# A place of its own in PSUM for the decay of each of two groups, instead of a ring of two

## The chip, the core and the metric

The kernel runs on one core of a Trainium2 chip, as one program. The time is device microseconds of that core; the metric is the median of several executions. One further execution was taken with the hardware profiler on, and what is said of instructions comes from that one.

## What is computed

Two layers work on 16 images of 64 x 64 pixels with 96 channels. The first layer normalizes by groups of channels, widens the image, applies two matrices with a square between them, and filters it back. The second layer is a state space layer, and nearly all of the time passes in its scan. Cut to what matters here:

```
delta = softplus(dts + bias)                    # per direction k, channel d, position l
h[l]  = exp(delta[l] * A[k,d,n]) * h[l-1] + delta[l] * u[l] * B[n,l]
y[l]  = sum over n of C[n,l] * h[l]             # 16 states n, 4 directions k, 192 channels d
```

`exp(delta * A)` is called the decay below, and `delta * u * B` the drive.

## The kernel before, in words

The scan is cut into *units*. A unit holds two groups, `e = 0` and `e = 1`; a group is 128 partitions (32 channels by 4 states) by 1024 positions in float32. Six blocks of channels, each with four sets of states (`j = 0` to `3`), make 24 units for a stretch of 1024 positions; four stretches, in two pairs of directions, make 192 units for an image, and 16 images make 3072 units. The units run in one long loop (L916), written out in full. The order of the instructions on each engine is the order in which the code names them (a manual schedule); the framework puts in the semaphores.

For each unit `n` and group `e`, these are the steps:

- `decay` (L785): ScalarE (ACT) writes `da = exp(delta * a)` into a tile of the PSUM pool `sc_aps`. A tile is 4 KB in each partition, two banks. Each `da` is a new tile.
- `drive` (L791): GpSimd (POOL) makes both groups' drive `b` in SBUF with one multiplication (L794). The tile `b` has four places.
- `recur` (L797): VectorE (DVE) runs the recurrence as one scan instruction over `da` and `b` (L803, or L805 where the direction is reversed). Its result goes either over `b` or over `da`.
- The result is multiplied by C. For group 0, DVE does it (L972, out of `da` into `b`). For group 1, POOL does it (L963, inside `b`), except in every fifth unit (`odd_here`, L948), where the scan's result stays in `da` and DVE does it (L954). These are called *fifth units* here. In some stretches a counter (`full_unit`) puts them closer together, and then leaves them out for a while.
- `keep` (L807): the last column is copied as the start of the next stretch, by DVE or ACT (L811).
- `read_out` (L813): TensorE (PE) sums over the states (L827).

In the loop the order for unit `n` is: scan of group 1, [fifth unit: DVE's multiplication], copy, **decay of (n+1, 1)**, POOL's multiplication of group 1, drive of n+2, scan of group 0, DVE's multiplication of group 0, copy, **decay of (n+1, 0)**. So while unit `n` is at work, the decays of unit `n+1` are made.

The PSUM pool `sc_aps` has two places (banks 2 and 3, banks 4 and 5). They are a common ring: each new `da`, of either group, takes a place that the framework picks when it lays out the program, and waits at run time for the last reader of the tile that had the place before.

Beside the scan, two *background* programs are put into the loop in slices: `front` of the next image (first layer, normalizations, convolution) and `finish` of the image before; and `project` of the next stretch. They use mostly PE and ACT, and a little DVE. In the last image there is no `front`.

Of the kernel before, what the change touches and what calls it, by code (L numbers as in the profile page):

```python
# [45 lines left out]
F32 = mybir.dt.float32  # L46
# [3 lines left out]
PSUM = bass.MemoryType.PSUM  # L50
# [12 lines left out]
T = 1024  # L63
# [17 lines left out]
def tile_two_blocks(  # L81
# [541 lines left out]
    def scan():  # L623


        with ExitStack() as es:
# [142 lines left out]
                    if (what, 0, j) not in bc:  # L769
                        bc[what, 0, j] = fetch_bc(ctxs[0], 0, j, what)  # L770
            banks.append(es.enter_context(tc.tile_pool(name="b_ps", bufs=2, space=PSUM)))
            aps = es.enter_context(tc.tile_pool(name="sc_aps", bufs=2, space=PSUM))
            yps = es.enter_context(tc.tile_pool(name="sc_yps", bufs=1, space=PSUM))
            gps = es.enter_context(tc.tile_pool(name="sc_gps", bufs=1, space=PSUM))

# [2 lines left out]
            def group(n, e):  # L778
                st, bi, _ = units[n]
                v, s0, r = blocks[bi]  # L780
                return 2 * steps[st][1] + r, s0 + e if v < 2 else 4 + e
# [2 lines left out]

            def decay(n, e):  # L785
                k, g = group(n, e)
                da = aps.tile([128, T], F32, name="da")
                nc.scalar.activation(da, deltas[n // NQ, e], AF.Exp, scale=a_s[:, k, g, units[n][2]:units[n][2] + 1])  # L788
                das[n, e] = da

# [121 lines left out]
            for e in range(2):  # L912
                decay(0, e)
            storing, credit = None, 0

            for n, (st, bi, j) in enumerate(units):  # L916
# [39 lines left out]
                if n < last:  # L956
                    decay(n + 1, 1)
# [16 lines left out]
                if n < last:  # L974
                    decay(n + 1, 0)
# [25 lines left out]
    with tc.manual_schedule():  # L1001
        with tc.tile_pool(name="first_ps", bufs=8, space=PSUM) as pool:
            banks.append(pool)
            for _ in front(0):
                pass
            banks.pop()
        scan()
        with tc.tile_pool(name="last_ps", bufs=8, space=PSUM) as pool:
            banks.append(pool)
            for _ in finish(B - 1):  # L1010
                pass
            banks.pop()
# [95 lines left out]
```

## Time and profile before

| | |
|---|---|
| median of 3 runs | 21318.96 us (21314.29 to 21335.73) |
| profiled execution, its own time | 21326.15 us |
| its span, first to last instruction | 21324.4 us |
| DVE busy | 19510.9 us, 91% |
| POOL busy | 19511.8 us, 91% |
| PE busy | 16949.4 us, 79%, at a mean granted clock of 0.859 |
| ACT busy | 13759.8 us, 65% |
| first scan starts, last scan ends | 495.9 us, 21158.7 us |

A row of the profile's groups gives the line, the engine, the operation, the tile written and the tiles read with their sizes, how often; then the busy time in us and the mean duration in ns; then the engine's idle time ahead of these instructions, and whose end it waited for. A row of the waits gives who waited for whom, the total in us, how often, and the longest. A row of the timeline gives start and duration in us, and in brackets the idle time ahead of it.

### The profile page before, as it was taken

How to read it: one execution, taken by the hardware profiler on the slowest of the kernel's cores; microseconds unless marked ns; L12 is line 12 of the kernel's file. 1: busy time of each engine (PE TensorE's matmuls, PEld its weight loads, DVE VectorE, ACT ScalarE, POOL GpSimd, SP SyncE). 2: the span in 40 equal slices, each digit the busy share in tenths (PEclk: the TensorE clock that was granted, in tenths of full speed). 3: DMA queues.
4: the chain of work that ended last, by engine and by line, in shares of the span. 5: the costliest groups of instructions: out<-in, count | busy, mean ns of one | idle time of the engine just before them, and what ended most of it. 6: DMA issues, size and time to landing. Idle time of an engine off the chain costs nothing. (4 is left out here: it accounts for less than half of the span.)

```text
span 21324.4 us, 273404 instructions
## 1 busy us (share of the span) xinstructions
PE 16949.4 (79%) x98988; PEld 7262.1 (34%) x98988; DVE 19510.9 (91%) x12983; ACT 13759.8 (65%) x20546; POOL 19511.8 (91%) x5538
## 2 busy tenths in 40 slices
PE   7876788887878778787887888878787787878855
PEld 4423324233343333324333342333433333243221
DVE  0999999999999999999999999999999999999997
ACT  4666666666666666666666666666666666666553
POOL 0999999999999999999999999999999999999996
PEclk8887888888889888898888888888898888988977
DMA  2565565655656566565665656556565665656654
GB/s 83 184 204 188 198 225 191 219 197 197 223 195 226 189 211 210 192 230 184 218 205 197 223 194 219 198 193 223 195 227 188 212 209 193 230 188 216 222 187 140
DMA packets 1855464, 4277.11 MB, mean 201 GB/s; under 512 B 449438, under 2 KB 548670, under 8 KB 1852062
## 3 DMA queue, kind: packets, MB, share of 16 engines
q1 hardware_dynamic: 1854110, 4259.62, 59.5%
q8 instruction: 781, 12.80, 0.3%
q14 instruction: 573, 4.69, 0.1%
HBM read 3380.58 MB, written 878.18 MB: 200 GB/s over the span
## 5 line engine op out<-in xcount | busy, mean ns | idle before, releaser
L794 POOL TENSOR_TENSOR b<-dtu,bt 128x2048 f32<-128x2048 f32 x3072 | 13908.5, 4537 | 593.7 <-DMA dtu<-dtu_d 468.4
L788 ACT ACTIVATE da<-delta,a_s 128x1024 f32<-128x1024 f32 x6144 | 6846.5, 1116 | 3074.8 <-DVE b L972 947.3
L963 POOL TENSOR_TENSOR b<-b,ct 128x1024 f32<-128x1024 f32 x2458 | 5809.4, 2363 | 1052.8 <-DVE new L811 786.2
L827 PE MATMUL y<-b,fold_s 128*32 128x256 f32 x49152 | 3871.0, 438 | 1122.9 <-DVE b L972 663.2
L972 DVE TENSOR_TENSOR b<-da,ct 128x1024 f32<-128x1024 f32 x3072 | 3756.5, 1223 | 91.8
L803 DVE TENSOR_TENSOR_SCAN da<-da,new,b 128x1024 f32<-128x1024 f32 x1383 | 3246.6, 2348 | 206.5 <-ACT da L788 198.8
L805 DVE TENSOR_TENSOR_SCAN da<-da,new,b 128x1024 f32<-128x1024 f32 x1361 | 3194.1, 2347 | 200.8 <-ACT da L788 188.6
L827 PEld LDWEIGHTS y<-b,fold_s 128*32 128x32 f32 x49152 | 1394.5, 119 | 3847.4 <-issue 1492.7
L805 DVE TENSOR_TENSOR_SCAN b<-da,new,b 128x1024 f32<-128x1024 f32 x943 | 2208.1, 2342 | 112.8 <-ACT da L788 81.0
L803 DVE TENSOR_TENSOR_SCAN b<-da,new,b 128x1024 f32<-128x1024 f32 x921 | 2156.3, 2341 | 10.5 <-ACT da L788 9.9
L811 ACT COPY new<-da 128x1 f32<-128x1 f32 x2764 | 432.9, 157 | 2568.8 <-DVE b L972 2178.3
L488 PE MATMUL c_ps<-xgp,wtap_s 96*64 96x512 f32 (+1 forms) x4608 | 1721.4, 632 | 180.4 <-ACT row L506 175.1
L697 PE MATMUL s<-w,ident_s 128*128 128x512 f32 x1530 | 1166.9, 854 | 722.4 <-ACT w L692 618.0
L371 PE MATMUL h_ps<-xu,w1t_s 96*128 96x500 f32 x1920 | 1053.7, 646 | 362.2 <-ACT sd L362 185.5
L383 PE MATMUL o_ps<-w2c_s,hsq 128*100 128x96 f32 x9600 | 1044.3, 267 | 207.3 <-ACT hsq L352 206.9
L805 DVE TENSOR_TENSOR_SCAN da<-da,b 128x1024 f32<-128x1024 f32 x482 | 1103.8, 2290 | 106.7 <-ACT da L788 98.9
L677 PE MATMUL s<-pr,dtw_s 128*128 128x512 f32 x1530 | 937.8, 697 | 302.0 <-ACT delta L703 214.5
L803 DVE TENSOR_TENSOR_SCAN da<-da,b 128x1024 f32<-128x1024 f32 x460 | 1053.5, 2290 | 107.1 <-ACT da L788 106.9
L383 PEld LDWEIGHTS o_ps<-w2c_s,hsq 128*100 128x100 f32 x9600 | 979.0, 179 | 447.8 <-ACT hsq L352 263.2
L820 PE MATMUL y<-y,ident_s 128*128 128x512 f32 x768 | 532.2, 781 | 627.3 <-ACT yt L838 501.7
L697 PE MATMUL s<-e,ident_s 128*128 128x512 f32 x1530 | 1014.5, 752 | 0.0
L488 PEld LDWEIGHTS c_ps<-xgp,wtap_s 96*64 96x64 f32 (+1 forms) x4608 | 582.9, 169 | 1115.4 <-issue 849.2
(143 smaller groups left out, 21887.5 us busy)
## 6 DMA issues: line engine op xcount, KB each, us to landing
dtu<-dtu_d SPq DMA_DIRECT2D x1536, 512.0 KB
delta<-delta_d SPq DMA_DIRECT2D x1536, 512.0 KB
bt<-rows SPq DMA_DIRECT2D x1024, 512.0 KB
ct<-rows SPq DMA_DIRECT2D x1024, 512.0 KB
u<-xs_d SPq DMA_DIRECT2D x893, 256.0 KB
dtu_d<-dtu SPq DMA_DIRECT2D x765, 256.0 KB
delta_d<-delta SPq DMA_DIRECT2D x765, 256.0 KB
xr<-in_x SPq DMA_DIRECT2D x768, 128.0 KB
```

The source lines that it names most:

```text
L371: nc.tensor.matmul(h_ps[j], lhsT=w1t_s[:, 128 * j:128 * (j + 1)], rhs=xu.rearrange("c p q -> c (p q)"), start=True, stop=True,)
L383: nc.tensor.matmul(o_ps[:, p, :], lhsT=hsq[j][:, UPS * p:UPS * (p + 1)], rhs=w2c_s[:, j, :], start=(j == 0), stop=(j == HB - 1),)
L488: nc.tensor.matmul(c_ps[p:p + n], lhsT=wtap_s[:, tap, 128 * i:128 * i + n], rhs=xgp[:, h0:h0 + 8, dx:dx + HW], start=(tap == 0), stop=(tap ...
L677: nc.tensor.matmul(s, lhsT=dtw_s[:, pair, v, :], rhs=pr, start=True, stop=True)
L697: nc.tensor.matmul(s, lhsT=ident_s, rhs=of, start=(k == 0), stop=(k == 3))
L788: nc.scalar.activation(da, deltas[n // NQ, e], AF.Exp, scale=a_s[:, k, g, units[n][2]:units[n][2] + 1])
L794: nc.gpsimd.tensor_mul(b, dtus[n // NQ], bt.unsqueeze(1).to_broadcast([128, 2, T]))
L803: nc.vector.tensor_tensor_scan(out, da, b, before, ALU.mult, ALU.add)
L805: nc.vector.tensor_tensor_scan(out[:, ::-1], da[:, ::-1], b[:, ::-1], before, ALU.mult, ALU.add)
L827: nc.tensor.matmul(y[32 * q:32 * q + 32, e, :], lhsT=fold_s, rhs=b[:, e, QT * q:QT * q + QT], start=(pair == 0 and j == 0 and e == 0), sto ...
L963: nc.gpsimd.tensor_mul(h, h, bc[1, r, j])
L972: nc.vector.tensor_mul(bs[n][:, 0, :], h, bc[1, r, j])
```

## The change

The pool `sc_aps` gets one place for each tag instead of two in all, and the tile `da` gets the tag `da0` or `da1` after its group. That is again two places of two banks. A decay of group 0 now always waits for the last reader of the decay of group 0 before it, and a decay of group 1 for that of group 1.

```diff
-            aps = es.enter_context(tc.tile_pool(name="sc_aps", bufs=2, space=PSUM))
+            aps = es.enter_context(tc.tile_pool(name="sc_aps", bufs=1, space=PSUM))
...
             def decay(n, e):
                 k, g = group(n, e)
-                da = aps.tile([128, T], F32, name="da")
+                da = aps.tile([128, T], F32, name="da", tag=f"da{e}")
                 nc.scalar.activation(da, deltas[n // NQ, e], AF.Exp, scale=a_s[:, k, g, units[n][2]:units[n][2] + 1])
```

## The prediction

> **What bounds the kernel now.** I read the page's first part, then the groups of instructions, the waits, the timeline of two neighbouring units, and the busy time by stretch. First the busy time:
>
> ```profile
> PE 16949.4 (79%) x98988; PEld 7262.1 (34%) x98988; DVE 19510.9 (91%) x12983; ACT 13759.8 (65%) x20546; POOL 19511.8 (91%) x5538
> ```
>
> DVE and POOL are equally busy. The scan lasts from 495.9 to 21158.7 us, 20663 us, so each of them is idle there for some 1150 to 1250 us; that is all that a better order could bring. Who waits for whom decides between the two:
>
> ```profile
> L803 DVE TENSOR_TENSOR_SCAN da<-da,new,b 128x1024 f32<-128x1024 f32 x1383 | 3246.6, 2348 | 206.5 <-ACT da L788 198.8
> L805 DVE TENSOR_TENSOR_SCAN da<-da,new,b 128x1024 f32<-128x1024 f32 x1361 | 3194.1, 2347 | 200.8 <-ACT da L788 188.6
> L805 DVE TENSOR_TENSOR_SCAN da<-da,b 128x1024 f32<-128x1024 f32 x482 | 1103.8, 2290 | 106.7 <-ACT da L788 98.9
> L803 DVE TENSOR_TENSOR_SCAN da<-da,b 128x1024 f32<-128x1024 f32 x460 | 1053.5, 2290 | 107.1 <-ACT da L788 106.9
> ```
>
> Ahead of scans that write over `da` (all of group 0, and group 1 of fifth units) DVE idles 198.8 + 188.6 + 98.9 + 106.9 = 593 us until a decay is ready: half of its idle time. It rarely waits for POOL's drive (under 60 us in all groups of scans). POOL does wait for DVE:
>
> ```profile
> POOL b L963 <- DVE new L811: 786.2, 367, 18.3
> ```
>
> So DVE sets the pace in most of the scan, and POOL follows close behind. The timeline shows how the 593 us come about (rows of DVE and ACT; between them others are left out):
>
> ```profile
> 9992.10 2.34 DVE L803 TENSOR_TENSOR_SCAN b<-da,new,b 128x1024 f32<-128x1024 f32 x1
> ...
> 9992.42 1.12 ACT L788 ACTIVATE da<-delta,a_s 128x1024 f32<-128x1024 f32 x1
> ...
> 9994.55 2.35 DVE L803 TENSOR_TENSOR_SCAN da<-da,new,b 128x1024 f32<-128x1024 f32 x1
> ...
> 9998.08 2.34 DVE L803 TENSOR_TENSOR_SCAN b<-da,new,b 128x1024 f32<-128x1024 f32 x1
> ...
> 9998.78 0.17 ACT L811 COPY new<-da 128x1 f32<-128x1 f32 x1
> 10000.45 0.15 DVE L811 COPY new<-b 128x1 f32<-128x1 f32 x1
> 10000.45 1.12 ACT L788 ACTIVATE da<-delta,a_s 128x1024 f32<-128x1024 f32 x1 [1.50 <-DVE b L803]
> ...
> 10001.60 2.36 DVE L803 TENSOR_TENSOR_SCAN da<-da,new,b 128x1024 f32<-128x1024 f32 x1 [1.00 <-ACT da L788]
> ```
>
> These are units 1405 and 1406. In the first, the decay of group 0 runs at 9992.42, beside the scan of group 1, and the scan of group 0 follows at once. In the second, ACT is free from 9998.95, yet waits 1.50 us for the end of the scan of its own unit's group 1. Only then does the decay of group 0 run, while DVE stands still for 1.00 us. In the program as built the reason is the place: in unit 1406 the decay of group 0 was given the place that group 1 of the *same* unit holds. I call such units crossed. Going through all 3070 units from the third on, 527 are crossed; in 2543 each group takes its own place.
>
> **The change, part by part.** *What moves.* The order on every engine is the same, and so are the waits of PE, POOL and SP. Of 6144 decays, 527 wait for something else: instead of the scan of (n, 1) they wait for DVE's multiplication of (n-1, 0) and ACT's copy behind it. The multiplication stands ahead of that scan on DVE, and the copy ahead of the decay on ACT. The other 527 decays that lose a foreign place, those of group 1 right behind a crossed decay, now wait for the scan of their own group in the unit before; but ACT comes to them only after the crossed decay, which had waited for that scan already. So no wait on another engine becomes later. On DVE 22 scans get an additional wait for an earlier instruction of DVE itself, on ACT some decays one for the copy just ahead; I cost both at nothing, since the 2543 units of the ordinary kind have the same wait.
>
> *What it removes.* DVE's idle time ahead of the scan of group 0, summed over the 527 crossed units, is 557.7 us (1.06 us each); over the 2543 others it is 31.6 us (0.01 us each). So the trace holds the changed state in four units of five, and at most 557.7 - 527 x 0.0124 = 551 us go.
>
> *What stays of it.* In 54 of the 527 (105.8 us) the decay starts more than 0.06 us after the scan's end: there it waits for `delta` from DRAM (14 units, 51.0 us) or ACT is still at other work. These stay. In the other 473 (451.9 us) the scan's end released it. For each I took the later of the end of ACT's instruction before it and the end of the multiplication of (n-1, 0), added 1.12 us, and compared with the end of the scan of group 1. Mostly the decay would be done in time; where ACT is behind, 89 us remain. That leaves 452 - 89 = 363 us.
>
> *What is late next: POOL.* DVE can only be ahead of POOL as far as the four places of `b` reach: in the long runs without a fifth unit, POOL's L963 starts 4.3 us behind the scan and the next drive ends 0.03 us before its scan. There POOL sets the pace, since POOL's ordinary unit takes 4.53 + 2.36 = 6.89 us (rows L794, L963) and DVE's 2.34 + 2.35 + 1.22 + 0.15 = 6.06. It catches up in fifth units (4.53 against 7.15). A bubble of DVE that goes is time won only where POOL idles nearby. In windows of 24 units, the sum of the smaller of the two (crossed idle time, POOL's idle time ahead of L963 and L794) is 480 of 551 us; in windows of 5 units 333 of 551. A lag of 4.3 us spans a few bubbles, so the truth lies between the shares 0.87 and 0.60; I take 0.8, nearer to the long window, as about nine in ten of the crossed units lie outside the long runs. 363 x 0.8 = 290 us.
>
> The SBUF row that speaks against it: 32 instructions of L237 (96x1) average 3614 ns and 16 of L260 2391 ns, where L259 of nearly the same shape takes 146 ns. With POOL idling less they could each wait out a whole drive: 32 x (4.53 - 3.61) + 16 x (4.53 - 2.39) = 64 us at most, nothing at least. I take nothing, as POOL is busy 94% of the scan already, and keep the 64 us for the upper end. The Trainium skill ("SBUF — State Buffer", Who interferes with whom) says that a DVE instruction with two SBUF inputs contends with a GpSimd instruction that reads SBUF, and with one SBUF input it does not; by that rule L237 and L260 pay, and the scans, with `da` in PSUM, never do. The trace agrees: the scans take 2.33 to 2.36 us throughout.
>
> *The sum.* 21326 - 290 = 21036 us for an execution like the profiled one; it lies 7 us above the median of the runs, so 21319 - 290 = 21029, rounded to **21030 us**, 1.4% less. A measurement of this kernel can tell about 0.2%, 43 us, from no change.
>
> **The rivals.**
>
> 1. *POOL hides nothing, ACT is never late: all 529 to 551 us go.* Then about 20780. For it: the ordinary units idle 0.01 us, and ACT, no longer held, would also be earlier for what follows. Against: 89 us were ACT's own lateness, and in the long runs POOL has no lead to give. Chance 0.10.
>
> 2. *POOL or ACT eats more than two thirds, but not all.* Two windows of units:
>
> ```profile
> core 0: us, PE busy (x) PEld busy (x) DVE busy (x) ACT busy (x) POOL busy (x), PEclk, DMA share, GB/s
> ...
> 9573.30:10866.00 1292.70, 1050.53 (x6169) 453.01 (x6170) 1210.84 (x807) 851.77 (x1277) 1214.08 (x345) 0.87 0.61 205
> 19922.00:21161.00 1239.00, 770.05 (x3916) 257.64 (x3920) 1207.13 (x800) 675.40 (x950) 1217.03 (x346) 0.76 0.55 188
> ```
>
> These are an image with `front` beside it and the last one without. The last has 8 crossed units instead of some 35 and takes 1239 us, with POOL busy 1217 of it. So an image can lose 54 us at most before POOL is full; 35 bubbles are 37 us of that, and the rest of the 54 belongs to waits that stay. If POOL's idle time is mostly of a kind that DVE's pace doesn't govern, a third of 290 us is left: 21220. Chance 0.08.
>
> 3. *POOL is the bound: no change.* POOL is busiest by 0.9 us, and if its own chain (drive, multiplication, drive) ran through, DVE's bubbles would only turn into waits for `b`: 21319, within 43 us. Against it stand the 786.2 us in which POOL waits for DVE's copy. The Trainium skill ("Perfetto Trace Analysis", Identifying the Most-Contended Engine) has the busiest engine optimized first; by it the change would be worth nothing here, which this row speaks against. Chance 0.06.
>
> 4. *PE becomes the bound: slower.* The granted clock is 0.87 in the one stretch and 0.76 in the other. If the closer packing brought the images with `front` down to 0.76, PE's 1050 us would become 1050 x 0.87 / 0.76 = 1202 of an image's 1275 (1293 less 18 won). POOL waits 98 us in all today for PE's sums to free a `b`; then a `read_out` in line behind a late `front` matmul would hold `drive`. It decides once PE's busy time and its waits pass 1293 us per image: 100 us more of waits would give 1202 + 100 = 1302, nine above today, 15 x 9 = 135 us, so 21450. Against it: the lower clock stands where PE has less to do, not more. Chance 0.03; with one more in 100 for what I don't see, slower has 0.04.
>
> **How the numbers follow.** The forecast's own case, 20840 to 21200, has 0.72. Its lower end is the 363 us without POOL's share plus most of the 106 us of other lateness (21319 - 480); its upper end is the share 0.60 on 363 us, less 64 us for L237 and L260, and rounded down by a quarter for ACT falling behind as DVE's pace rises (21319 - 120). The range adds a little of rivals 1 and 2 at each end: 20820 to 21210. Faster than 21276 is 0.72 + 0.10 + 0.08 = 0.90; within 43 us 0.06; slower 0.04.
>
> **What would show it.** In the changed profile the idle time of the four groups that write over `da` should fall from 593 to about 200 us or less; no decay should show an idle time ended by the scan of group 1 of its own unit; the timeline of unit 1406 should look like that of 1405. DVE's waits for POOL's drive (L794) should rise from under 60 us to 100 or more, and POOL's wait for DVE (786.2 us) should fall by some 300. DVE and POOL busy times and the scan's duration stay within a few tenths of a per cent. I am wrong about the mechanism if the 593 us go and the span stays (rival 3), or if they stay; wrong about the size if POOL's wait falls by less than 150 us.

## The result, and the profile after

The changed kernel takes 21086.31 us (median of 4 runs, 21075.62 to 21088.51), against 21320.87 us for the kernel before (4 runs). The ratio is 0.9888, with a 95% interval of 0.9871 to 0.9905: 234.6 us less (234 in what follows), where 290 us were forecast and 20820 to 21210 us was the range. The profiled execution has a span of 21083.6 us, 240.8 us shorter than before.

The busy line of the page of the profile after:

```profile
PE 16908.7 (80%) x98988; PEld 7230.6 (34%) x98988; DVE 19569.4 (93%) x12983; ACT 13780.9 (65%) x20546; POOL 19498.8 (92%) x5538
```

The groups of scans that write over `da`, from the groups of DVE after (busy us, mean ns, idle us ahead of them and whose end it waited for):

```profile
L803 DVE TENSOR_TENSOR_SCAN da<-da,new,b 128x1024 f32<-128x1024 f32 x1383 | 3245.3, 2347 | 72.7 <-ACT da L788 57.2 <-POOL b L794 13.3
L805 DVE TENSOR_TENSOR_SCAN da<-da,new,b 128x1024 f32<-128x1024 f32 x1361 | 3193.0, 2346 | 99.7 <-ACT da L788 77.0 <-POOL b L794 21.0
...
L805 DVE TENSOR_TENSOR_SCAN da<-da,b 128x1024 f32<-128x1024 f32 x482 | 1103.5, 2289 | 53.0 <-ACT da L788 43.1 <-POOL b L794 9.2 <-ACT new L811 0.6
L803 DVE TENSOR_TENSOR_SCAN da<-da,b 128x1024 f32<-128x1024 f32 x460 | 1053.0, 2289 | 36.8 <-ACT da L788 34.8 <-POOL b L794 0.9 <-ACT new L811 0.2
```

The idle time that ends with a decay has fallen from 593 us to 57.2 + 77.0 + 43.1 + 34.8 = 212 us. The scans themselves last what they lasted, to a few ns. But DVE is busy for 58.5 us more, and parts of the idle time now end with POOL's drive. In the list of waits, POOL still waits for DVE, 158 us less than the 786.2 us of before, and PE waits longer for POOL's product:

```profile
POOL b L963 <- DVE new L811: 628.6, 296, 14.1
PE y L827 <- POOL b L963: 167.1, 136, 5.3
```

Before, that row of PE was:

```profile
PE y L827 <- POOL b L963: 133.8, 110, 5.5
```

The timeline of the same two units, 1405 and 1406, in the profile after:

```profile
9868.05 2.34 DVE L803 TENSOR_TENSOR_SCAN b<-da,new,b 128x1024 f32<-128x1024 f32 x1
...
9868.35 1.12 ACT L788 ACTIVATE da<-delta,a_s 128x1024 f32<-128x1024 f32 x1
...
9870.49 2.35 DVE L803 TENSOR_TENSOR_SCAN da<-da,new,b 128x1024 f32<-128x1024 f32 x1
...
9874.01 2.34 DVE L803 TENSOR_TENSOR_SCAN b<-da,new,b 128x1024 f32<-128x1024 f32 x1
...
9874.92 1.12 ACT L788 ACTIVATE da<-delta,a_s 128x1024 f32<-128x1024 f32 x1
...
9876.46 2.35 DVE L803 TENSOR_TENSOR_SCAN da<-da,new,b 128x1024 f32<-128x1024 f32 x1
```

Both units now look alike: the decay of group 0 starts while the scan of group 1 runs (9874.92, the scan ends at 9876.35), and DVE goes from scan to scan.

An account of the 240.8 us, from the groups of DVE in both traces (every gap is counted, also those under 0.15 us, which the rows of the profile leave out of their releasers). L702 is a multiplication of `project` that reads PE's sums, L578 one of `finish`; L237 and L260, which come up below, are small instructions of `front`, on 96x1 and 96x96 numbers.

| DVE | before, us | after, us | difference |
|---|---|---|---|
| all scans' idle time ended by a decay | 718.2 | 339.2 | -379.0 |
| all scans' idle time ended by POOL | 60.3 | 109.7 | +49.4 |
| busy | 19510.9 | 19569.4 | +58.5 |
| L702's idle time, nearly all until PE is done | 319.8 | 345.7 | +25.9 |
| L578's idle time, nearly all until ACT is done | 111.7 | 120.9 | +9.2 |

The sum is -236 us; 5 us are spread over the rest. In DVE's busy time the one group that grew is L237, from 115.6 to 195.0 us (records of neighbouring instructions overlap a little, so that the busy time grows by less). Its row before and after:

```profile
L237 DVE TENSOR_TENSOR nb<-nmean,rg 96x1 f32<-96x1 f32 x32 | 115.6, 3614 | 303.4 <-ACT rg L234 295.4 <-ACT new L811 8.1
```

```profile
L237 DVE TENSOR_TENSOR nb<-nmean,rg 96x1 f32<-96x1 f32 x32 | 195.0, 6095 | 301.9 <-ACT rg L234 294.2 <-ACT new L811 7.6
```

So the ring's bubbles (the idle time of DVE ahead of crossed scans) went as counted, and 143 us came back in four places. That L702's part comes from POOL, by way of PE's longer wait for POOL's product (133.8 to 167.1 us), is argued from these sums and not shown one by one. Where in an image they came back I took from the starts of the first scan of each part, for the 14 images from the second to the fifteenth:

| units of an image | idle time in crossed units, before and after | time won |
|---|---|---|
| 0 to 71 | 235.9, 58.7 us | 180.1 us |
| 98 to 149 | 242.3, 114.9 us | 17.7 us |
| the others | 40.1, 0.8 us | 12.8 us |

In the first part (units 0 to 71) as much time was won as idle time went (177 us gone, 180 won). In the later part (units 98 to 149) 127 us went and 18 were won. This is a balance of unlike places. In units 96 to 101, 18 us of waits for a decay went, but L237 grew by 52 us, and these units took 35 us longer. In units 120 to 125, 28 us went, and the waits for POOL's drive grew by 28 us and that of L702 by 18. In units 132 to 137, 28 us went and 30 were won.

POOL's idle time fell by about what was won: from 394 to 221 us in the first part, from 591 to 574 us in the later one (14 images). So POOL had more idle time in the later part than in the first, and hardly any of it went.

### The profile page after: what moved, and what is told of

Same layout as the page of the kernel before. It is cut to its first block, busy times and chain, and to the rows that moved or that the text cites. A ratio compares the mean times of both kernels' runs of the same rounds, so it can differ in the third digit from the quotient of the medians.

```text
span 21083.6 us, 273452 instructions
## 1 busy us (share of the span) xinstructions
PE 16908.7 (80%) x98988; PEld 7230.6 (34%) x98988; DVE 19569.4 (93%) x12983; ACT 13780.9 (65%) x20546; POOL 19498.8 (92%) x5538
## 5 line engine op out<-in xcount | busy, mean ns | idle before, releaser
L963 POOL TENSOR_TENSOR b<-b,ct 128x1024 f32<-128x1024 f32 x2458 | 5797.1, 2358 | 836.9 <-DVE new L811 628.6
L803 DVE TENSOR_TENSOR_SCAN da<-da,new,b 128x1024 f32<-128x1024 f32 x1383 | 3245.3, 2347 | 72.7 <-ACT da L788 57.2
L805 DVE TENSOR_TENSOR_SCAN da<-da,b 128x1024 f32<-128x1024 f32 x482 | 1103.5, 2289 | 53.0 <-ACT da L788 43.1
L803 DVE TENSOR_TENSOR_SCAN da<-da,b 128x1024 f32<-128x1024 f32 x460 | 1053.0, 2289 | 36.8 <-ACT da L788 34.8
```

What stands on the lines that cost most here:

```text
L803: nc.vector.tensor_tensor_scan(out, da, b, before, ALU.mult, ALU.add)
L805: nc.vector.tensor_tensor_scan(out[:, ::-1], da[:, ::-1], b[:, ::-1], before, ALU.mult, ALU.add)
L963: nc.gpsimd.tensor_mul(h, h, bc[1, r, j])
```

## The experiments

The theory was: a bubble of DVE is time only where POOL has idle time near it; elsewhere POOL is late already, and DVE meets POOL's lag (how far POOL is behind DVE's scans) at the next place where it depends on it. The first half of it does not fit the sums above, as POOL had idle time near the bubbles of both parts; the second half, that POOL takes the time back at the places where DVE depends on it, is what e3 to e6 test. The first rival was that each crossed unit costs the same, 234 / 527 = 0.44 us; further rivals belong to single runs.

To cross chosen units, the places were written out. `PLACE` takes the other place for group 0 of a unit unless the unit is in `CROSSED`; with all 527 units in it, the places are those of the kernel before, one by one:

```diff
+CROSSED = set(...)
+PLACE = {(0, 0): 0, (0, 1): 1, (1, 1): 1}
+for _n in range(1, 3072):
+    PLACE[_n, 0] = PLACE[_n, 1] if _n in CROSSED else 1 - PLACE[_n, 1]
+    PLACE[_n + 1, 1] = 1 - PLACE[_n, 0]
...
-                da = aps.tile([128, T], F32, name="da", tag=f"da{e}")
+                da = aps.tile([128, T], F32, name="da", tag=f"da{PLACE[n, e]}")
```

**e1, the 272 units of the first part crossed again.**

> Own places as in the changed kernel, except that the 272 units that were crossed in units 0 to 71 of an image (of 527) are crossed again. Theory 1 (a crossed unit costs time only where POOL idles nearby): these are the stretches that won nearly all, 180 us over 14 images in the two traces, so about 195 us over the whole come back: 21086 + 195 = 21280 us. Rival (each crossed unit costs the same, 234 / 527 = 0.44 us): 21086 + 272 x 0.44 = 21207 us.

Measured: 21291.74 us (10 runs), 0.9988 of the kernel before (0.9979 to 0.9997). 205 us are back, 0.75 us for each unit. The rival's 21207 us is out of reach.

**e2, the 215 units of the later part crossed again.**

> Own places, except that the 215 units that were crossed in units 98 to 149 of an image are crossed again. Theory 1: this stretch won only 18 us over 14 images although 157 us of DVE's idle time went there, since a second loss took it back (DVE's L237 behind a busier POOL, waits for the drive): 21086 + 20 = 21105 us, and L237's mean falls back from 6.1 us towards 3.6. Rival (same price everywhere): 21086 + 215 x 0.44 = 21181 us.

Measured: 21086.37 us (0.9889, 0.9874 to 0.9904), the changed kernel's time to a tenth of a microsecond. These 215 crossed units cost nothing in sum (that the two agree so closely is chance, as the runs of e2 lie between 21072.88 and 21099.99 us). The profile says how; its groups of the two instructions that gave way, and one group of scans:

```profile
L805 DVE TENSOR_TENSOR_SCAN da<-da,new,b 128x1024 f32<-128x1024 f32 x1361 | 3193.5, 2346 | 174.1 <-ACT da L788 159.2 <-POOL b L794 10.9 <-ACT new L811 2.6
...
L702 DVE TENSOR_TENSOR dtu<-s,u 128x512 f32<-128x512 f32 x765 | 520.7, 681 | 279.7 <-PE s L697 278.3 <-DMA dtu<-dtu_d 0.3 <-issue 0.3
L237 DVE TENSOR_TENSOR nb<-nmean,rg 96x1 f32<-96x1 f32 x32 | 140.8, 4400 | 302.5 <-ACT rg L234 294.9 <-ACT new L811 7.6
```

Against the changed kernel, the idle time ended by a decay is up by 126 us over all scans (465.3 against 339.2; the first row shows 82 of it). In return L237 is down from 195.0 to 140.8 us, L702's wait from 345.7 to 287.9 and the scans' wait for POOL from 109.7 to 88.4: 133 us. DVE waits about the same time in sum, only for something else. The two runs together show that the price of a crossed unit depends on its place: 0.75 us on average in one part, none on average in the other. Within the later part it differs as much: against the changed kernel, in 14 images, units 96 to 101 take 35 us less and units 120 to 125 19 us less, but units 132 to 137 30 us more. The expected times came from the same two profiles, so these runs confirm where the time is won, and not yet why. (The 157 us of idle time in e2's expectation are not what the traces give: it is 127 us in 14 images, 140 us in all 16.)

**e3 and e4, L237 on ACT.** The largest single group that grew was L237, a multiplication of 96 numbers at which DVE and POOL meet. The timelines of DVE and of POOL around the same instruction of the program (the 26th of 32), in the kernel before:

```profile
15429.10 2.29 DVE L237 TENSOR_TENSOR nb<-nmean,rg 96x1 f32<-96x1 f32 x1 [0.22 <-ACT rg L234]
...
15424.04 4.54 POOL L794 TENSOR_TENSOR b<-dtu,bt 128x2048 f32<-128x2048 f32 x1
15429.01 2.36 POOL L963 TENSOR_TENSOR b<-b,ct 128x1024 f32<-128x1024 f32 x1 [0.43 <-POOL b L794]
15431.33 9.01 POOL L794 TENSOR_TENSOR b<-dtu,bt 128x2048 f32<-128x2048 f32 x2
```

and in the kernel after:

```profile
15244.41 12.32 DVE L237 TENSOR_TENSOR nb<-nmean,rg 96x1 f32<-96x1 f32 x1 [0.22 <-ACT rg L234]
...
15240.96 4.53 POOL L794 TENSOR_TENSOR b<-dtu,bt 128x2048 f32<-128x2048 f32 x1
15245.43 2.38 POOL L963 TENSOR_TENSOR b<-b,ct 128x1024 f32<-128x1024 f32 x1
15247.74 8.96 POOL L794 TENSOR_TENSOR b<-dtu,bt 128x2048 f32<-128x2048 f32 x2
```

Before, POOL had begun its L963 0.09 us ahead of L237, and both ended together (15431.37 and 15431.39). After, POOL was a drive behind, had three more instructions in line without a gap, and L237 ended at 15256.73, with the last of them (15256.70). So DVE can wait for several instructions of POOL here. In 30 of the 32 places POOL was at work, and there, in both kernels, L237 ended 0.01 or 0.02 us after an instruction of POOL. After the change POOL then had nothing ready each time, for 2.5 us or more: DVE paid POOL's whole lag. Before, that was so 24 times; the other six times, the one shown here among them, POOL's next instruction followed without a gap. What let L237 through there stays open. Both kernels were run with that line on ACT:

```diff
-        nc.vector.tensor_mul(nb, nmean, rg)
+        nc.scalar.activation(nb, nmean, AF.Identity, scale=rg)
```

> The kernel before, with its places kept unit by unit, but L237 (nb = nmean * rg, 32 times) on ACT instead of DVE. Its 115.6 us on DVE (3.6 us each) become about 0.2 us each on ACT. Theory: DVE had to wait for POOL there, so 80 to 110 us go: about 21225 us. Rival (POOL sets the pace anyway at those places): no change, 21320 us.

> The changed kernel, with L237 on ACT as well. There L237 took 195.0 us (6.1 us each), 79 us more than before the change. Theory (L237 took back part of the gain): 21086 less 150 to 190 us, 20900 to 20935 us, and the distance to e3_nb_ring is 234 + 79 = about 310 us. Rival (the lead that POOL owes is only paid elsewhere, as waits for the drive): the distance stays at 234 us, about 20990 us.

Measured: e3 (places as before) 21183.84 us, 0.9937 (0.9921 to 0.9954); e4 (own places) 20929.54 us, 0.9815 (0.9801 to 0.9830). e3 gains 135 us, more than the 115.6 us that L237 had on DVE; e4 gains 157 us, less than its 195.0 us. The distance between the two is 254 us, near the rival's 234 and not my 310. L237 was a place where POOL's lag was collected. Without it, e4 pays elsewhere: against e3 its scans wait 117.0 us instead of 57.0 for POOL, and L702 351.9 instead of 322.8. L260, the other small instruction that the prediction had named, pays too. It had 38.3 and 38.1 us in the kernels before and after, and its rows in e3 and then in e4 are:

```profile
L260 DVE TENSOR_TENSOR lin<-lin,ident_s 96x96 f32<-96x96 f32 x16 | 52.9, 3303 | 0.0
```

```profile
L260 DVE TENSOR_TENSOR lin<-lin,ident_s 96x96 f32<-96x96 f32 x16 | 73.3, 4582 | 0.0
```

From e3 to e4, in 14 images, units 96 to 101, where L237 had grown by 52 us, win 17 us instead of losing 35; units 120 to 125, with the waits for the drive and of L702, lose 18 us instead of 9.

**e5 and e6, POOL relieved.** If it is POOL's lag, then less work for POOL must bring out the whole of the bubbles. In both kernels, half of one multiplication on POOL is left out:

```diff
-                    nc.gpsimd.tensor_mul(h, h, bc[1, r, j])
+                    nc.gpsimd.tensor_mul(h[:, 0:T // 2], h[:, 0:T // 2], bc[1, r, j][:, 0:T // 2])
```

> The kernel before with POOL relieved: L963 multiplies 512 of the 1024 columns only (the other half of group 1 keeps the unmultiplied scan, so the output is not the reference's). POOL's unit falls from 6.9 to about 5.7 us, below DVE's 6.1. Places as in the kernel before. DVE loses its waits for the drive (60 us) and part of L237's 116 us: about 21150 to 21250 us by both theories.

> The changed kernel with POOL relieved in the same way (half of L963's columns left out). Theory (POOL, by its lag and through L237, ate what is missing between the 379 us of idle time that went and the 241 us of the span): with POOL out of the way the distance to e5_half_ring is the full idle time, 350 to 390 us. Rival (ACT's own lateness or other waits ate it): the distance stays at about 235 us.

Measured: e5 (ring) 21159.65 us, 0.9924 (0.9909 to 0.9938); e6 (own places) 20763.40 us, 0.9737 (0.9721 to 0.9753). The distance is 396 us instead of 234, a little above the 350 to 390 expected. All idle time ended by a decay falls by 352 us from one to the other, L702's by 14. DVE's busy time falls by 26 us, though the durations of its instructions sum to the same: without a gap, the records of neighbours overlap more. The units that had taken time back no longer do: in 14 images units 96 to 101 win 18 us and units 120 to 125 16. The groups of POOL's second multiplication, e5 and then e6:

```profile
L963 POOL TENSOR_TENSOR b<-b,ct 128x512 f32<-128x512 f32 x2458 | 3125.6, 1272 | 3374.6 <-DVE b L803 1579.4 <-DVE new L811 903.7 <-DVE b L805 369.6
```

```profile
L963 POOL TENSOR_TENSOR b<-b,ct 128x512 f32<-128x512 f32 x2458 | 3122.7, 1270 | 2994.9 <-DVE b L803 1327.6 <-DVE new L811 837.5 <-DVE b L805 358.0
```

POOL now idles 3.0 to 3.4 ms ahead of it, 2.5 to 2.9 ms of that until DVE is done; the scans wait 3.6 and 2.6 us for it, and L237 takes 0.8 and 1.0 us. With POOL out of the way the change is worth about what DVE's bubbles sum to, and a little more by the overlap. What is missing in the full kernel is POOL's.

**e7 to e10, another share of the work.** In the kernel before, every fifth unit gives the multiplication of group 1 to DVE. If POOL now sets the pace more often, the balance should move (L237 stays on ACT):

```diff
-SHARE = 5
+SHARE = 6        # e7;  4 in e8 and e9 (e9 with the common ring), 3 in e10
```

> As e4_nb_own, but every sixth instead of every fifth unit leaves group 1's multiplication to DVE: 102 multiplications go from DVE (1.07 us more there than the copy it saves) to POOL (2.36 us). If DVE sets the pace nearly everywhere: up to 110 us faster than e4, 20820 us. If POOL sets it: up to 241 us slower, 21170 us. By the traces both do, in turns (DVE in units 0 to 71, POOL in units 150 to 168), so between 20880 and 21000 us.

> As e4_nb_own, but every fourth unit: 154 multiplications go from POOL to DVE. DVE gets 165 us more work, POOL 362 us less. If DVE sets the pace: up to 165 us slower than e4, 21095 us. If POOL sets it: faster. By the traces DVE sets it in the larger part, so 20950 to 21090 us.

Measured: e7 20958.11 us (0.9834, 0.9817 to 0.9850), 29 us more than e4 and within what was expected. e8 20868.95 us (0.9791, 0.9776 to 0.9805): 61 us *faster* than e4, where I had expected it slower. DVE's busy time rises only from 19411.5 to 19504.3 us, as L260 falls from 73.3 to 21.8 us, and its idle time shrinks by more: the waits for a decay from 348.4 to 309.9 us, those for POOL from 117.0 to 49.6 us, that of L702 from 351.9 to 291.2. So POOL set the pace in more of the kernel than the traces had told me.

> As e8_share4 (every fourth unit, L237 on ACT), but with the common ring of two. As built, 455 units are crossed instead of 527. If the ring's bubbles and POOL's lag stand in for one another, then with POOL relieved the bubbles cost more each than in e3 against e4 (254 us for 527, 0.48 us each): 455 x 0.65 = about 300 us above e8, 21165 us. If POOL's work plays no part in it: 455 x 0.48 = 219 us above e8, 21090 us.

> As e8_share4, but every third unit: 256 more multiplications go from POOL to DVE, 274 us more work for DVE. If POOL still set the pace with every fourth, faster than e8; if DVE does now, up to 274 us slower. DVE should: 20950 to 21140 us.

Measured: e9 21139.02 us (0.9913, 0.9896 to 0.9929), 270 us above e8 for 455 crossed units, 0.59 us each. That lies between the two expectations (219 and 300 us) and does not decide between them; it fits a price that rises when POOL has less to do, but other units are crossed here. e10 21187.91 us (0.9938, 0.9923 to 0.9952), 319 us more than e8, where at most 274 us more were expected. From e8 to e10 the span grows by 310 us and DVE's busy time by 313 us: DVE is the bound with every third unit. The multiplications (L954) alone took 313 us more, and L260 25 us. e8 is the best of the row.

e8 beats both kernels: own places, L237 on ACT, every fourth unit on DVE, 2.1% less than the kernel before and 1.0% less than the changed one.

## Why the prediction was right, point by point

- *The crossed units.* Right. Before, 473 decays of group 0 started within 0.06 us after the end of their own unit's scan of group 1; after, one does, and none waited for it. The idle time of the 527 units fell from 557.7 to 178.4 us, 379 us, where 363 were worked out. The 178 us that stay are the two kinds named: 46 us in waits for `delta`, and 132 us ahead of decays to which ACT comes late. The four groups of scans show 212 us, close to the 200 forecast.
- *No wait on another engine becomes later.* Right as far as the traces go: POOL's wait for PE's sums, which rival 4 feared, fell from 98.3 to 87.6 us, and PE's mean granted clock is unchanged (0.86 against 0.859). PE waits longer for POOL's product, but with POOL relieved (e5) that wait is 16.0 us, so it is POOL's lag rather than a changed order.
- *POOL's share, 0.8.* This is the mis-sized term: 234 / 379 = 0.62 was measured, next to the share of the short windows (0.60) and not of the long ones (0.87). I took a bubble for time won wherever POOL idles nearby. In units 98 to 149 POOL idled 591 us, more than the bubbles' 242, and its median lag behind the scans was 1.1 us where 4.3 us is all that the four places of `b` allow (14 images); still only 18 of the 127 us that went were won. POOL idle somewhere near is not enough: the time is lost again at the places where DVE depends on POOL, L237 and the units around 120. That the short windows came out right is therefore luck, as far as the runs tell. A share by part (all of it in units 0 to 71, little in units 98 to 149) would have been better than one for all; e1 and e2 confirm it.
- *L237 at nothing, 64 us at most for it and L260.* Wrong for L237: it alone went from 115.6 to 195.0 us, +79 us. This is part of what the share of 0.62 lacks and not a loss beside it. The bound assumed that it waits out one drive; the timeline shows 12.32 us behind three of POOL's instructions after the one in progress. L260 did not change (2391 and 2379 ns), until L237 was gone in e4 (4582 ns). The scans, which the prediction has at 2.33 to 2.36 us, took 2.27 to 2.36 us and did not change. The Trainium skill ("SBUF — State Buffer", Who interferes with whom) has such an instruction of two SBUF inputs contend with GpSimd's reads; that much the trace bears out, and that the wait runs over several of them in a row is what this case adds. e3 and e4 show that its growth is a place of payment more than a cost of its own: without it the change is worth 254 us instead of 234, not 310.
- *Rival 1* (all 529 to 551 us go) fell in both halves: POOL hid a part, and ACT was late for 132 us. With less work for POOL, e5 against e6, the part that POOL hid came out. *Rival 2* (a third of 290 us is left) fell with 234 us. *Rival 3* (no change) fell for the whole, but in sum it held for 215 of the 527 crossed units, those of e2.
- *The range.* Its lower end goes 480 us down, but the two terms that it names, 363 and 106 us, sum to 469. The result was not near it.
- *What would show it.* DVE's waits for the drive were to rise from under 60 to 100 us or more: from 57.7 to 101.3 us by the rows of the groups (60.3 to 109.7 with the gaps under 0.15 us). POOL's wait for DVE was to fall by some 300 us: 158 us, just above the 150 us named as the sign of a wrong size, and the size was indeed the weak point.

## What to carry to other kernels

Two streams that share a ring of buffers can end up in one another's place; look for the transfer of a place from one stream to the other within the same step, and give each stream its own. When two engines are equally busy, price a bubble place by place: follow it to the next instruction that depends on the other engine, and ask whether that engine will be done by then. Idle time of the other engine somewhere near does not answer it. After such a bubble is gone, look at the balance between the two engines again; here that was worth another 1.0%: 157 us for L237's move and 61 us for the share.

## What the runs showed of the hardware that was not expected

A DVE instruction on 96 x 1 numbers (L237, both inputs in SBUF) took up to 12.32 us while POOL ran its instructions without a gap, and ended with the last of them. In 30 of its 32 places, in both kernels, it ended 0.01 or 0.02 us after an instruction of POOL, though not always after the last of a row. With POOL relieved (e5) the same group averages 839 ns. On ACT it takes 280 ns.
